# Score maxima read from two banks each by ScalarE and VectorE, and row tiles of 13 sequences turned by VectorE and DRAM

## The chip, the cores and the metric

The kernel runs on one core of a Trainium2 chip. The engines of a core are TensorE (PE), VectorE (DVE), ScalarE (ACT), GpSimd (POOL) and SyncE (SP, which here only issues DMAs); they run side by side and wait for each other by semaphores. The metric is the device time of one execution in microseconds (us), as the median of several runs; lower is better. Everything is computed in fp32.

## The reference

One post-norm decoder layer over 16 sequences of 512 tokens with 256 channels, and a context of 64 tokens with 128 channels for each sequence. `ln` is a layer norm without weights. Cut to what matters:

```python
def reference(x, ctx, ...):
    x = ln(x + hyena(x))            # gated long convolution, then an MLP of width 672
    x = ln(x + xattn(x, ctx))       # causal self-attention plus cross-attention, 16 heads of 16
    x = ln(x + ffn(x))              # 256 -> rank 64 -> 1024 -> rank 64 -> 256
    return x

def hyena(u):
    z = causal_conv3(rmsnorm(u) @ in_proj_w.T)
    x2, x1, v = split(z)
    y = (long_conv(x1 * v) + x1 * v * D_skip) * x2
    y = y @ out_proj_w.T + u
    zm = rmsnorm(y)
    return y + (gelu(zm @ l1_w.T) * (zm @ l2_w.T)) @ l3_w.T

def xattn(x, ctx):
    att  = where(causal, q @ k.T / 4, -inf)          # q, k, v from x, per head
    attc = qc @ kc.T / 4                              # qc from x, kc and vc from ctx
    return (softmax(att) @ v + softmax(attc) @ vc) @ Wp + bp

def ffn(x):
    return gelu((x @ U1) @ V1 + b1) @ U2 @ V2 + b2
```

Each softmax needs the maximum of its row of scores, over the allowed keys, before the exponentials are taken.

## The kernel before

**Two plans.** The kernel is written as a list of operations (`plan.op`), each with the engines that may run it, an assumed cost, an assumed latency of a DMA (`lat`), a priority, and the buffers that it reads and writes. `Plan.schedule` goes through an assumed time and gives each engine its order; a buffer is taken from its pool when its first operation starts. The table `RANKS` shifts priorities of single kinds of operations; `HOLD` and `STAY` weigh changes of the TensorE array's tiling. The result is a fixed order for each engine. On the chip every engine works through its own order, and a late operand holds up whatever comes behind it on that engine. A first plan (up to about 440 us) does the convolutions of all sequences; a second does everything else, sequence by sequence, overlapped.

**One sequence in the second plan.** `first_block` multiplies the convolution by its gate, projects it and makes the tile `y1`; the MLP follows, then a layer norm. `attention` makes keys, queries and values, the maxima, the sums, divides, projects and normalises. `ffn` is the last block. A tile of rows has tokens on its partitions, `[128, 4, 256]`; a matmul wants channels there. So each of the three blocks first turns its tile: `transposed` (L402) makes 8 PE transposes of 128x128 into two PSUM buffers of the pool `mm` (three in all), and ScalarE or VectorE copies each into the tile `xT` (three in all). Three turns a sequence: of `y1` (the trace names it y), of `x_` for attention and of `x_` for ffn (named xt, or early for every fourth or so).

**The tiling of the array.** PE runs either as 128*128 or cut into strips; a matmul of 128*32 uses a quarter of the columns, and four of them with different quarters run side by side. Score fills use 32*64 (eight side by side). Operations marked `flex` take the tiling that is on. Every fp32 matmul shows up in the trace as two. Transposes need 128*128.

**The scores.** There is one PSUM buffer `scores` of four banks, one for each head of a group; a sequence has four groups. For the maxima (`maxima`, L1472) a group makes three fills, (1, 0), (2 and the context of 3) and (3), by query block. For sequences 2 to 12 VectorE then adds the mask on the diagonal blocks in PSUM (L1548) and reduces all four banks there (L1580). For the five sequences of `COPIED` (0, 1, 13, 14, 15) ScalarE copies the whole fill to an SBUF tile `ex` (L1525), GpSimd masks it (L1532) and VectorE reduces it from there; in sequences 0, 1 and 15 the fill and the copy are made in halves (`HALVED_MAX`). The same buffer then holds the second computation of the scores, keys on the partitions, which ScalarE turns into exponentials (`sums`, L1611; context, L1688 on): five fills for a pair of groups and two for the context. The maxima of two groups are turned by PE (`max turn`, L1591) and added to the queries as an extra row (`shifted`, L1600).

**Other parts that the change touches.** The sums go to DRAM (`dn`), are divided by way of SP's queue and the SBUF tiles `nd` (three), and come back (L1765 on). `ffn` brings 256 channels to rank 64 (`rank`, L1852; both halves of the partitions get the same 64 ranks of all 512 tokens), then `hidden` (L1870) and GELU (L1876), 8 matmul groups of 64 rows. The context's values (`ctx v`, L1381) are made from a copy of the context side by side with itself (`twice`).

Of the kernel before, what the change touches and what calls it, by code (L numbers as in the profile page):

```python
# [27 lines left out]
    "context.sum ctx": -2000,  # L28
    "divided.num from": -400,
    "ffn.gelu": 4000,  # L30
    "ffn.hidden": -2000,
    "ffn.norm": 5000,
    "ffn.rank": -1000,
    "ffn.stats": 2000,
    "ffn.turn": -100,
    "ffn.wide": 4000,
    "first.load x": 2000,
    "first.out": -2000,
    "first.residual": -2000,
    "maxima0.max": -7000,  # L40
    "maxima1.copy": 1000,
    "maxima1.mask copy": -1000,
    "maxima1.max": -900,
    "mlp.down": 1000,
    "mlp.shift": -3000,
    "queries0.proj out": -320,
    "queries1.proj": 20,
    "queries1.proj out": -3000,
    "result.norm": 13000,
    "result.shift": 10000,  # L50
    "result.stats": 3000,
    "result.tokens": 14000,
    "shifted.max turn": 400,
    "shifted.shifted": 1000,
    "sums.exp": -1000,
    "sums.fill": -3000,
    "sums.sum": -2000,
    "sums.sum out": 2000,
    "values.ctx keys": 400,
    "values.ctx v out": 1000,  # L60
    "values.turn": -1000,
    "values.v": 100,
}
SLOT_OF = (1, 0, 2, 3)


class Buf:


    def __init__(self, cls):  # L70
        self.cls, self.seen, self.left, self.slot, self.t = cls, [], 0, None, None

# [27 lines left out]
class Plan:  # L100
# [55 lines left out]
    def matmul(self, out, weights, moving, **kw):  # L156

        rows, cols = self.now
        n = weights.shape[-1]
        for c in range(0, n, cols):  # L160
            cs = slice(c, min(c + cols, n))
            self.nc.tensor.matmul(out[cs], weights[:, cs], moving, **kw)  # L162
# [97 lines left out]
def decoder_layer(  # L260
# [60 lines left out]
    mask_qk = const.tile([P, P], F32, name="mask_qk")  # L321
    nc.gpsimd.memset(mask_qk, 0.0)
    nc.gpsimd.affine_select(
        out=mask_qk, in_=mask_qk, compare_op=ALU.is_ge, fill=NEG, base=0,
        pattern=[[-1, P]], channel_multiplier=1,
    )
# [100 lines left out]

    R8 = 8
# [5 lines left out]
    with ExitStack() as front:  # L434
# [40 lines left out]
        ramp_i = fp_.tile([P, P], I32, name="ramp_i")  # L475
        steps = fp_.tile([P, P], F32, name="steps")
        ramp = fp_.tile([P, P], F32, name="ramp")
        back = fp_.tile([P, 1], F32, name="back")
# [472 lines left out]
        u1_s = weights.tile([P, KD, 2, RANK], F32, name="u1_s")  # L951
        v1_s = weights.tile([P, NH // 2 * P], F32, name="v1_s")
        v2_s = weights.tile([P, D], F32, name="v2_s")
        v1_halves = v1.rearrange("r (p s n) -> s r p n", s=2, n=P)
        for n in range(2):
            half = bass.ts(n, RANK)
            fetch(u1_s[:, :, n, :], u1.rearrange("(k p) f -> p k f", p=P))
            fetch(v1_s[half, :].rearrange("r (p n) -> r p n", n=P), v1_halves[n])
            fetch(v2_s[half, :], v2)
        u1_s = u1_s.rearrange("p k s f -> p k (s f)")  # L960
# [110 lines left out]
        "row": tiles(kept, "row", 6, [P, T]),  # L1071
        "q": tiles(kept, "q", 11, [P, T]),
        "keys": tiles(kept, "keys", 5, [P, TC + T]),
        "kcs": tiles(kept, "kcs", 2, [P, 2, G, TC]),
        "ctx2": tiles(kept, "ctx2", 2, [CC, 2, TC]),
# [5 lines left out]
        "dk": dks,  # L1081
        "junk": tiles(kept, "junk", 1, [P, D]),
# [9 lines left out]
    for t in pool["maxes"]:  # L1092
        nc.gpsimd.memset(t, 0.0)

    plan = Plan(pool, 13890, 6870, nc, RANKS)
# [73 lines left out]
    def first_block(b, after):  # L1169
# [56 lines left out]
        if b:  # L1226
            scale_ops(y1, sq, p0, "ACT")
            zT = transposed(y1, lambda t: t, p0)
# [15 lines left out]
        for f in range(NF):  # L1244
            halves = []
            for w in (w_l1, w_l2):
                ps = Buf("mm")
                for k in range(KD):

                    def mm(e, f=f, w=w, k=k, ps=ps):  # L1250
                        plan.matmul(
                            ps.t, w[:, k, bass.ts(f, P)], zT.t[:, k, :], start=(k == 0), stop=(k == KD - 1)
# [24 lines left out]
        def mm_e(e, ps=ps):  # L1277
            for n, w in enumerate((w_l1, w_l2)):
                for k in range(KD):
                    for c in range(NT):  # L1280
                        plan.matmul(
                            ps.t[bass.ts(c, FE), bass.ts(n, P)], w[:, k, NF * P :], zT.t[:, k, bass.ts(c, P)],
# [32 lines left out]
    def attention(b, x_):  # L1315
# [3 lines left out]
        xT = transposed(x_, lambda t: t, p0)  # L1319
# [701 lines left out]
```

## Time and profile before

| | us |
|---|---|
| median of three runs (2019.52, 2025.77, 2025.89) | 2025.77 |
| the profiled execution, its own time | 2020.74 |
| its span, first to last instruction | 2018.6 |
| PE idle in 0 to 440 us (front plan) | 43.7 |
| PE idle in 500 to 1700 us | 4.3 |
| PE idle in 1700 to 1900 us | 5.2 |
| PE idle in 1900 to 2019 us | 17.7 |
| granted TensorE clock, mean | 0.992 |
| DMA: bytes moved, mean rate | 183.92 MB, 91 GB/s |

The idle times are a window's length less PE's busy time in it. The page gives the busy time of each engine, then 40 slices of the span, the DMA queues, the chain that ended last, and the costliest groups. In a group's line stand the source line, the engine, the operation, what is written and read, the count, the busy time in us, the mean of one in ns, and after the second bar the idle time before it. Nearly all matmuls have the line L162, a helper, so they are told apart by tile names. A "busy" PE holds overlapping and modelled ends; the start of one piece to the start of the next is the better measure of its cost. From 500 to 1700 us the kernel is in a steady state, in which a sequence takes 103.8 us.

### The profile page before, as it was taken

The page shows a single profiled execution, that of the slowest core. Times are in us where ns is not written, and L with a number is a line of the kernel's source. Part 1 is how long each engine was busy: PE and PEld are TensorE (multiplying, and loading weights), DVE is VectorE, ACT ScalarE, POOL GpSimd, SP SyncE. Part 2 cuts the span into 40 slices and gives each one's busy share as a digit, 9 for nine tenths or more (in the row PEclk, how much of TensorE's full clock was granted, in tenths as well). Part 3 has the DMA queues.
Part 4 walks back from the last instruction along what each step waited for, and adds up shares of the span by engine and source line. Part 5 has one row for each costly group of instructions (what it writes and reads, how often), then busy time and mean ns, then how long its engine had stood idle before and what let it go on. Part 6 is the DMA issues. An engine that isn't in the chain of part 4 may idle for free. (4 is left out here: it accounts for less than half of the span.)

```text
span 2018.6 us, 63455 instructions
## 1 busy us (share of the span) xinstructions
PE 1946.6 (96%) x28134; PEld 864.7 (43%) x28134; DVE 1320.4 (65%) x1907; ACT 1046.4 (52%) x1478; POOL 767.2 (38%) x1036
## 2 busy tenths in 40 slices
PE   7999978999999999999999999999999999999997
PEld 4445645444444443434343434343434343434442
DVE  7987542556576757676767667676767575656564
ACT  6863521566536362636363545444444546656774
POOL 7685622243423242414242423333332324424442
PEclk9999989999999999999999999999999999999999
DMA  5375871031304131313132222222231313131200
GB/s 191 123 212 172 274 256 48 13 104 38 116 21 133 29 121 41 113 50 112 51 102 60 94 69 81 82 74 89 61 102 52 106 38 108 28 103 39 83 23 32
DMA packets 115043, 183.92 MB, mean 91 GB/s; under 512 B 13393, under 2 KB 62034, under 8 KB 114642
## 3 DMA queue, kind: packets, MB, share of 16 engines
q1 hardware_dynamic: 113234, 177.26, 27.9%
q8 instruction: 220, 3.60, 0.7%
q10 hardware_dynamic: 1536, 2.62, 0.4%
q14 instruction: 53, 0.43, 0.1%
HBM read 111.09 MB, written 68.76 MB: 89 GB/s over the span
## 5 line engine op out<-in xcount | busy, mean ns | idle before, releaser
L1611 ACT ACTIVATE ex<-scores 128x2048 f32<-128x2048 f32 (+1 forms) x228 | 362.7, 1607 | 181.3 <-PE scores L162 177.7
L1659 POOL TENSOR_SCALAR_AFFINE_SELECT ex<-ex 128x512 f32<-128x512 f32 x256 | 158.6, 634 | 498.9 <-ACT ex L1611 498.8
L162 PE MATMUL mm<-xT,w_l 128*32 128x512 f32 (+2 forms) x2940 | 316.5, 540 | 0.0
L1580 DVE TENSOR_REDUCE maxes<-scores 128x8 f32<-128x512 f32 (+4 forms) x264 | 311.1, 1220 | 4.5
L162 PE MATMUL scores<-keys,q 32*64 32x192 f32 (+5 forms) x5696 | 218.1, 407 | 9.5 <-ACT ex L1525 5.0
L162 PE MATMUL scores<-q,keys 32*64 32x256 f32 (+3 forms) x4480 | 179.9, 420 | 6.2 <-ACT ex L1611 4.8
L1548 DVE TENSOR_TENSOR scores<-scores,mask_qk 128x1024 f32<-128x1024 f32 x132 | 115.6, 875 | 106.1 <-PE scores L162 105.3
L162 PEld LDWEIGHTS scores<-keys,q 32*64 32x64 f32 x5696 | 102.9, 131 | 172.2 <-DVE maxes L1580 52.9
L162 PEld LDWEIGHTS mm<-xT,w_l 128*32 128x32 f32 (+1 forms) x2940 | 92.7, 111 | 184.6 <-issue 175.0
L162 PE MATMUL av<-ex,va 128*32 128x512 f32 (+3 forms) x2048 | 169.0, 437 | 0.1
L162 PE MATMUL mm<-w_l,gT 128*32 128x256 f32 (+1 forms) x2032 | 159.7, 381 | 0.0
L562 DVE SCALAR_TENSOR_TENSOR frow<-fmm,cw,frow 128x511 f32<-128x511 f32 x192 | 140.5, 743 | 26.0 <-ACT frow L554 21.7
L1580 DVE TENSOR_REDUCE maxes<-ex 128x4 f32<-128x512 f32 (+3 forms) x120 | 140.6, 1211 | 17.9 <-POOL ex L1532 13.7
L1804 POOL TENSOR_TENSOR nd<-nd,nd 128x1024 f32<-128x1024 f32 x30 | 71.2, 2373 | 204.5 <-DMA nd<-di 204.5
L1525 ACT COPY ex<-scores 128x1024 f32<-128x1024 f32 (+1 forms) x96 | 114.3, 1228 | 66.7 <-PE scores L162 55.9
L547 PE MATMUL fmm<-fx,inw 128*128 128x512 f32 x312 | 142.2, 598 | 0.0
L361 DVE COPY row<-av 128x512 f32<-128x512 f32 x66 | 45.6, 690 | 138.8 <-PE av L162 137.7
L1876 ACT ACTIVATE row<-mm,b_s 128x512 f32<-128x512 f32 x124 | 78.9, 685 | 102.4 <-PE mm L162 99.5
L162 PE MATMUL mm<-xT,wqc_s 128*32 128x512 f32 (+1 forms) x796 | 125.4, 595 | 0.0
L162 PEld LDWEIGHTS scores<-q,keys 32*64 32x64 f32 x4480 | 79.5, 131 | 98.6 <-ACT ex L1611 45.0
L162 PEld LDWEIGHTS mm<-w_l,gT 128*32 128x32 f32 (+1 forms) x2032 | 89.3, 117 | 68.8 <-issue 34.5
L1263 ACT ACTIVATE row<-mm 128x512 f32<-128x512 f32 x80 | 47.9, 599 | 123.7 <-PE mm L162 112.0
(201 smaller groups left out, 2954.6 us busy)
## 6 DMA issues: line engine op xcount, KB each, us to landing
dn<-row SPq DMA_DIRECT2D x120, 256.0 KB
keys<-dk SPq DMA_DIRECT2D x64, 256.0 KB
nd<-dn SPq DMA_DIRECT2D x30, 512.0 KB
nd<-di SPq DMA_DIRECT2D x30, 512.0 KB
fx<-hpad SPq DMA_DIRECT2D x28, 512.0 KB
early<-gates SPq DMA_DIRECT2D x16, 512.0 KB
early<-yconv SPq DMA_DIRECT2D x32, 256.0 KB
dk<-row SPq DMA_DIRECT2D x32, 256.0 KB
```

The source lines that it names most:

```text
L162: self.nc.tensor.matmul(out[cs], weights[:, cs], moving, **kw)
L361: nc.vector.tensor_copy(dst, src)
L547: nc.tensor.matmul(ps.t, inw[:, k, bass.ts(m, P)], xT.t[:, k, :], start=(k == 0), stop=(k == KD - 1))
L562: lambda e, lag=lag: nc.vector.scalar_tensor_tensor(t.t[:, lag:], ps.t[:, 0 : T - lag], cw[:, m, 2 - lag : 3 - lag], t.t[:, lag:], ALU.mul ...
L1263: lambda e, pa=pa, ge=ge: nc.scalar.activation(ge.t, pa.t, AF.Gelu_apprx_tanh),
L1525: lambda e, sc=sc, both=both, cols=cols: nc.scalar.copy(both.t[:, :, cols], sc.t[:, :, cols]),
L1548: nc.vector.tensor_tensor(diag, diag, mask, ALU.add)
L1580: nc.vector.tensor_reduce(dst, src, AX.X, ALU.max, negate=True)
L1611: lambda e: nc.scalar.activation(ex.t.rearrange("p (r n) -> p r n", r=HPG)[:, :, cols], sc.t[:, :, cols], AF.Exp, scale=scale),
L1659: lambda e, ex=ex, at=at: nc.gpsimd.affine_select(out=ex.t.rearrange("p (r n) -> p r n", r=HPG)[:, :, at : at + P], in_=ex.t.rearrange("p ...
L1804: lambda e, nums=nums, inv=inv: nc.gpsimd.tensor_tensor(nums.t, nums.t, inv.t, ALU.mult),
L1876: lambda e, f=f, s=s, bank=bank, dst=hT[s]: nc.scalar.activation(dst.t, bank(s), AF.Gelu_apprx_tanh, bias=b1_s[:, f : f + 1]),
```

## The change

1. **Turns.** `turned` (new) replaces `transposed` for the three tiles of sequences 2 to 14: VectorE turns 32x32 blocks into an `xT` tile, one DMA writes it to DRAM (`turns`), and four DMAs read it back so that each 32-channel strip lies on its partitions. The tokens of such a tile lie in runs of 32; `tokens` and `columns` give the matmuls the access pattern. The maxima's own turn stays on PE, since the last entry of `TURNED` is empty.
2. **Maxima.** All 16 sequences take one form. Of the four banks of a fill, ScalarE copies two to an `nd` tile, GpSimd masks them and VectorE reduces them from there; VectorE reads the other two in PSUM: it adds the mask on the way into a small tile `part`, takes the maximum of what is off the diagonal, and then reduces `part`. `declare_no_dep` lets both engines read at once, since the banks differ. No fill is halved any more. The order of the first fill is (0, 1).
3. **ffn.** `rank` gives each half of the partitions its own half of the tokens (256 columns in place of 512); `hidden` and GELU then work in pieces of 256 columns.
4. **Context values.** Half as many columns, no copy `twice`.
5. **Plan.** New `RANKS`, `HOLD` 13570 and `STAY` 8710 (before 13890 and 6870), other assumed DMA latencies; pool `row` 5 (before 6), `q` 10 (before 11), `part` new, `ctx2` gone.

```diff
+    def turned(src, view, prio):
+        dst, via = Buf("xT"), Buf("turns")
+        dst.by_rows = True
+        def blocks(e):
+            nc.vector.transpose(
+                dst.t.rearrange("p k n -> p (k n)").rearrange("p (e k c i) -> p c k e i", e=NT, k=KD, c=NT),
+                view(src.t).rearrange("p c (k e j) -> p c k e j", k=KD, e=NT),
+            )
+        def there(e):
+            nc.sync.dma_start(out=via.t, in_=dst.t.rearrange("p k n -> p (k n)"))
+        def back(e):
+            rows = via.t.rearrange("(a j) (e n) -> e j a n", j=SLOT, e=NT)
+            for q in range(NT):
+                part = dst.t[bass.ts(q, SLOT)].rearrange("p k n -> p (k n)").rearrange("p (a n) -> p a n", a=NT)
+                nc.sync.dma_start(out=part, in_=rows[q])
+        plan.op("blocks", "DVE", dve(KD * T), blocks, prio, r=[src], w=[dst])
+        plan.op("blocks to", "SP", 0.6, there, prio, r=[dst], w=[via], lat=1.9)
+        plan.op("blocks from", "SP", 2.4, back, prio, r=[via], w=[dst], lat=3.5)
+        return dst
...
+    def tokens(xT, k, c=None):
+        if not xT.by_rows:
+            return xT.t[:, k, :] if c is None else xT.t[:, k, bass.ts(c, P)]
+        t = xT.t.rearrange("p k n -> p (k n)").rearrange("p (a k c i) -> p k c a i", a=NT, k=KD, c=NT)[:, k]
+        return t if c is None else t[:, c]
...
-        "row": tiles(kept, "row", 6, [P, T]),
-        "q": tiles(kept, "q", 11, [P, T]),
+        "row": tiles(kept, "row", 5, [P, T]),
+        "q": tiles(kept, "q", 10, [P, T]),
+        "part": tiles(kept, "part", PARTS, [P, HPG // 2, 2 * P]),
...
-            zT = transposed(y1, lambda t: t, p0)
+            zT = (turned if b in TURNED[0] else transposed)(y1, lambda t: t, p0)
...
-        xT = transposed(x_, lambda t: t, p0)
+        xT = (turned if b in TURNED[1] else transposed)(x_, lambda t: t, p0)
...
-            for use in (((1, TC), (0, TC)), ((2, TC), (3, None)), ((3, 0),)):
+            for use in (((0, TC), (1, TC)), ((2, TC), (3, None)), ((3, 0),)):
...
+                plan.op(
+                    "half", "ACT", act(two * T), lambda e, sc=sc, half=half: reading(sc, e, nc.scalar.copy(half.t, sc.t[:, two:])),
+                    prio - 6, r=[(sc, 1)], w=[half],
+                )
...
+                plan.op("half mask", "POOL", 0.4 * blocks, masked, prio - 6, w=[half])
...
+                    reading(sc, e, nc.vector.tensor_tensor(to, on_diagonal(sc.t[:, here]), m, ALU.add))
+                plan.op("mask", "DVE", dve(blocks * two * P), mask, prio - 5, r=[(sc, 0)], w=[part])
...
-                        nc.vector.tensor_tensor(diag, diag, mask, ALU.add)
-                    plan.op("mask", "DVE", dve((2 if use[0][0] == 1 else 1) * HPG * P), masked, ps_ - 5, w=[sc])
...
-                plan.matmul(ps.t, u1_s[:, k, :], x2T.t[:, k, :], start=(k == 0), stop=(k == KD - 1))
+                for n in range(P // SLOT):
+                    half, cols = n // 2, bass.ts(n % 2, SLOT)
+                    if x2T.by_rows:
+                        to = ps.t[bass.ts(n, SLOT), 0:D].rearrange("p (c a i) -> p c a i", c=2, a=NT)
+                        moving = tokens(x2T, k)[:, 2 * half : 2 * half + 2]
+                    else:
+                        to, moving = ps.t[bass.ts(n, SLOT), 0:D], tokens(x2T, k)[:, bass.ts(half, D)]
+                    nc.tensor.matmul(to, u1_s[:, k, cols], moving, start=(k == 0), stop=(k == KD - 1))
...
-    COPIED = (0, 1, B - 3, B - 2, B - 1)
-    HALVED, HALVED_MAX = (0, 1, B - 1), (0, 1, B - 1)
+    TURNED = *(range(2, B - 1) for n in range(3)), ()
+    HALVED = (0, 1, B - 1)
```

VectorE's instructions per group in the new form, with the elements per partition: first fill: mask 512, off-diagonal 256, context 256, own 512 (these read PSUM or `part`), then from `nd` context 256, own 256 and 512; second fill: 256, 512, 256, 256, then 256 and 768; third fill: 256, 768, 256, then 1024.

## The prediction

> **What bounds the kernel now.** I read the page's busy line first, then the windows by stage, then the same window for the tile `scores` alone, then PE's timeline, then the groups by shape.
>
> ```profile
> PE 1946.6 (96%) x28134; PEld 864.7 (43%) x28134; DVE 1320.4 (65%) x1907; ACT 1046.4 (52%) x1478; POOL 767.2 (38%) x1036
> ...
> 500.00:1700.00 1200.00, 1195.73 (x18172) 496.00 (x18165) 809.04 (x1145) 572.58 (x734) 393.35 (x529) 1.00 0.26 79
> ...
> 1900.00:2019.00 119.00, 101.28 (x1662) 42.00 (x1646) 71.91 (x143) 76.28 (x105) 41.54 (x70) 0.97 0.09 29
> ```
>
> In the windows the columns are length, then busy time of PE, PEld, DVE, ACT and POOL. TensorE is busy for all but 4 us of the 1200 us in the middle; VectorE has 391 us free there, ScalarE 627. The other view, same window, `scores` alone:
>
> ```profile
> 500.00:1700.00 1200.00, 307.71 (x7104) 124.32 (x7104) 426.62 (x396) 269.93 (x154) 1.00 0.26 79
> ```
>
> `scores` is one buffer, so its writers and readers take turns: 307.7 + 426.6 + 269.9 = 1004 us, 84% of the stretch. With a hand-over on each side of a fill, this turn-taking (I call it the ring) is nearly as full as PE. A shorter PE alone would soon meet it. PE's timeline shows what a piece of work costs from its start to the next start:
>
> ```profile
> 916.88 1.07 PE L162 MATMUL mm<-wp_s,xT 128*32 128x256 f32 x16
> 917.76 0.61 PE L162 MATMUL av<-ex,va 128*32 128x256 f32 x8
> ...
> 922.08 1.09 PE L410 MATMUL mm<-ident,xt 128*128 128x128 f32 x8
> 923.10 1.12 PE L162 MATMUL scores<-keys,q 32*64 32x320 f32 x32
> 924.15 1.07 PE L162 MATMUL mm<-xT,wk_s 128*32 128x512 f32 x8
> ...
> 942.67 0.64 PE L162 MATMUL mm<-wcv_s,ctx 128*32 128x256 f32 x8
> 943.24 0.66 PE L410 MATMUL mm<-ident,y 128*128 128x128 f32 x4
> 943.73 0.60 PE L162 MATMUL mm<-wp_s,xT 128*128 128x256 f32 x2
> 944.17 0.60 PE L410 MATMUL mm<-ident,y 128*128 128x128 f32 x4
> 944.61 0.60 PE L162 MATMUL mm<-wp_s,xT 128*128 128x256 f32 x2
> 945.13 1.12 PE L162 MATMUL scores<-q,keys 32*64 32x384 f32 x32
> ...
> 976.61 1.92 PE L162 MATMUL mm<-xT,u_s 128*32 128x512 f32 x16
> 978.35 1.90 PE L162 MATMUL mm<-xT,w_l 128*32 128x512 f32 x16
> ```
>
> **PE, removed.** (1) Turns. Sequences 2 to 14 lose their three tile turns: 39 tiles of eight transposes. Eight take 1.02 us (922.08 to 923.10), four take 0.49 and 0.44 (943.24, 944.17). 39 x 1.02 = 39.8 us. From below 39 x 0.88 = 34; from above by the busy unions of the three groups at L410 (28.0 + 18.4 + 10.6 us for 192 + 120 + 64, 0.152 each) 312 x 0.152 = 47. (2) Changes of the array's tiling. Two full-width pieces take 0.44 us before another full one, 0.52 before a 32*64 fill (944.61): 0.08 us for a change. A turned tile no longer pulls the array to 128*128: 39 x 0.1 = 4 us, between 0 and 8. (3) `rank`: 16 matmuls of 512 columns, 1.74 us (976.61 to 978.35), become 16 of 256, 0.88 us (916.88 to 917.76): 16 x 0.86 = 13.8 us; if the new form needs 1.05, 11. (4) `ctx v`: 0.57 us (942.67 to 943.24) for 8 of 256 columns becomes 8 of 128; 32 such take 0.90 us from 960.55, so 0.23 and a change: about 0.32. 16 x 0.25 = 4 us, between 0 and 5.
>
> **PE, added.** (5) `hidden` (16 x 512 in 1.02 us, 981.23 to 982.25) streams the same columns in twice as many matmuls. Fills of 16 x 512 (900.31 to 901.35) and 32 x 256 (912.05 to 913.10) take 1.04 and 1.05 us: I take 0; by the longest fill in the chain's list (1.20 us against 1.13) 64 x 0.1 = 6 us. (6) A by-rows tile is streamed in runs of 32 elements, which no row shows. Nearest: L664 streams 32 columns in runs of 8 in 199 to 201 ns, L756 48 contiguous ones in 207; at 0.85 ns a column (512 in about 0.435 us) 32 should take 193. 7 ns on 4 runs is 1.75 ns a run; 416 operations (20 of the MLP and 12 projections in 13 sequences) of two passes and 16 runs each would pay 23 us. I take 0, since such short matmuls show mostly their fixed part.
>
> Sum: 39.8 + 4 + 13.8 + 4 = 61.6 us. The last window has 18 us of idle PE, so the two turns and three ranks that fall there (4.6 us) give nothing: 57.
>
> **The maxima.** They use no PE, but they free the ring. Durations from the groups by shape: VectorE 0.41 us for 256 elements (the statistics at L1108), 0.69 for 512, 1.215 for 1024, so 0.155 fixed.
>
> ```profile
> L1548 DVE TENSOR_TENSOR scores<-scores,mask_qk 128x512 f32<-128x512 f32 x88 | 61.4, 698 | 65.8 <-PE scores L162 65.8
> ...
> L1580 DVE TENSOR_REDUCE maxes<-scores 128x4 f32<-128x1024 f32 x44 | 53.5, 1215 | 0.0
> ...
> L1525 ACT COPY ex<-scores 128x1024 f32<-128x1024 f32 x72 | 69.5, 1015 | 39.0 <-PE scores L162 28.2 <-issue 10.5 <-ACT row L363 0.3
> ```
>
> Before, VectorE held the buffer per group for 1.23 + 2 x 0.70 of masks and 2.29 + 1.75 + 2 x 0.69 + 1.215 + 0.68 of maxima: 9.95 us over three fills. Now it reads two banks: 0.70 + 0.41 + 0.41, 0.41 + 0.69 + 0.41, 0.41 + 0.95: 4.4 us, beside ScalarE's 1.02 a fill. That is 5.5 us a group, 22 us a sequence, off the ring. A sequence takes 103.8 us (the fill `scores<-q,kcs` starts at 834.03 and 937.84), PE wants about 99 after the change, the ring about 68. The later half on SBUF brings VectorE's total back to 10.0 us a group. The five sequences that were copied whole paid 7.27 (145.3 us over 20 groups): 20 x 2.7 = 55 us more. With 39 block turns (1.2 us by the 1024 row; a 32x32 turn has no row, I allow 0.7, the 512 row, to 3) and some 55 of 78 copies at 0.69 gone, VectorE ends near 1385 of 1965 us. ScalarE: 192 x 1.02 for 114 us of old copies, and 128 more GELU starts at about 0.3: +110 us, to 1155. GpSimd: 256 masks of 0.35 for 80 of 0.63: +40. I cost these at nothing, because PE's work covers them: in the steady stretch VectorE has 33 us in 100 free, ScalarE 52. Without cover the 55 us of the five sequences would show.
>
> The rows themselves first: a group's VectorE instructions go from 9 to 17, at 0.155 us fixed eight more are 1.2 us, 79 us in 64 groups, all inside the 10.0 above. [...]
>
> **What moves.** A turned tile now goes by VectorE, one write and four reads on SP's queue.
>
> ```profile
> 936.98 0.61 SPq L1453 DMA_DIRECT2D dk<-row  x1
> 941.28 0.32 SPq L1459 DMA_DIRECT2D keys<-dk  x1
> ...
> 963.66 0.61 SPq L1796 DMA_DIRECT2D nd<-di  x1
> ...
> 970.25 2.37 POOL L1804 TENSOR_TENSOR nd<-nd,nd 128x1024 f32<-128x1024 f32 x1 [4.07 <-DMA nd<-di]
> ```
>
> A 256 KB store lets the dependent read go 4.3 us later; a 512 KB read is used 6.6 us after its issue. So 1.2 + 4.3 + 1.3 (four issues at 0.32) + 4.3 to 6.6: 11 to 13 us from normed rows to turned tile, against 2.1 now (922.08 to 924.15). The issues (39 x 5 at 0.32 to 0.62, 62 to 121 us) go to SP, which mostly waits; but `blocks from` waits there for its store, with the key reads, the sums' stores and the divisions' reads behind it. A key read pushed late delays a maxima fill, a sums' store keeps a `row` buffer, of which one fewer is left. The plan books 2.5 and 5.9 us and can lay other PE work under it. I allow 2 us more PE waiting in all.
>
> 57 - 2 = 55 us. The profiled execution took 2020.74 us around a span of 2018.6; less 55 is 1965.7. The three runs shown were 2019.52 to 2025.89, median 2025.77, 5 us above it. I say 1966.
>
> **Rivals.** (A) The ring stays as full: ScalarE's copy queues behind other work, or lacks an `nd` buffer. For it: a division holds two of three `nd` from 950.84 to 973.98, 23 us twice a sequence, and half a fill needs 1.02 + 0.35 + 1.1 there before the next can be copied. If holds stay near 3.3 us a fill, the ring keeps its pace and PE idles where it was relieved: 2021, no change. Against: only half of the time, and the hold would be 2.5 us even then. 6%. (B) PE's costs of (5) and (6) are real, and the low ends of (1) to (4): 34 + 11 - 6 - 23 = 16, or half-way 30: 1991. Still faster. 10%. (C) Slower: the 9 to 11 us of added latency before the keys' projection is not covered. For it: the first use comes 0.1 us after the copies now, and keys, maxima and shifts follow. Price: 13 sequences by what is exposed; it decides from 57 / 13 = 4.4 us. With 6 us: 78 - 57 = 21 slower, 2042. Against: in the 17 us after 922.08 the list has projections, sums and `out` of another sequence, and the ring has gained 22 us a sequence. 14%.
>
> **Chances.** Main case 70%, A 6, B 10, C 14. About 0.3%, 6 us, can be told from no change here: faster 80%, same 6%, slower 14%. Range: upward 75 + 6 (PE's waits for L1525's copies) gives 1940; downward 16 gives 2005. I say 1938 to 2004.
>
> **What would show it.** No L410 turns between about 500 and 1800 us; PE still above 98% busy there; fills of `scores` in the maxima about 3 us apart when PE allows, not 4.6 to 5.5; the 512-column rows unchanged at 0.43 us a pass. Wrong: PE waits for `xT` from DMA, or `scores` fills waiting for ACT or `nd`; DVE above 90% in a window.

## The result and the profile after

The changed kernel takes **2114.57 us** (median of 4 runs, 2104.94 to 2117.21) against 2025.83 for the kernel before, run on the same chip: ratio 1.0429, 95% interval 1.0381 to 1.0477. It is 89 us slower. The forecast was 1966 us, with 80% on faster; both the sign and the range were wrong.

The page of the changed kernel, its busy time and three groups (busy us, mean ns of one | idle time before them and what ended it):

```profile
PE 1927.2 (91%) x28726; PEld 840.5 (40%) x28726; DVE 1359.1 (64%) x2493; ACT 1114.0 (53%) x1649; POOL 815.9 (39%) x1196
...
L158 PE MATMUL mm<-xT,w_l 128*32 128x512 f32 (+2 forms) x2874 | 322.4, 555 | 63.9 <-DMA xT<-turns 58.9
L1573 ACT COPY nd<-scores 128x1024 f32<-128x1024 f32 x192 | 194.6, 1014 | 347.1 <-PE scores L158 303.1
L1580 POOL TENSOR_SCALAR_AFFINE_SELECT nd<-nd 128x256 f32<-128x256 f32 x256 | 101.4, 408 | 591.9 <-ACT nd L1573 591.7
```

The window of 500 to 1700 us, all engines (length, then PE, PEld, DVE, ACT, POOL, the granted clock, DMA share and GB/s):

```profile
500.00:1700.00 1200.00, 1108.81 (x17927) 451.71 (x17908) 771.95 (x1443) 640.68 (x848) 436.11 (x652) 0.97 0.34 102
```

and the same window for the tile `scores` alone:

```profile
500.00:1700.00 1200.00, 296.90 (x6755) 118.35 (x6736) 176.63 (x346) 378.00 (x272) 0.97 0.34 102
```

Two things stand side by side. The ring did become emptier, as forecast: fill, VectorE and ScalarE hold the one buffer for 852 us of the stretch (296.9 + 176.6 + 378.0, and some of it overlaps now), before 1004 in turn. Yet PE, busy for all but 4 us of this stretch before, is idle for 91 us of it. Its waits, over the whole span (us in total, times, longest), and below them what the second one was before:

```profile
PE mm L158 <- DMA xT<-turns: 58.9, 9, 10.8
PE scores L158 <- ACT ex L1691: 31.4, 38, 2.1
PE av L158 <- POOL ex L1739: 16.7, 7, 4.2
...
PE scores L158 <- DMA keys<-dk: 6.2, 2, 5.7
```

```profile
PE scores L162 <- ACT ex L1611: 5.9, 7, 1.2
```

The nine waits on `xT<-turns` are `w_l`, the first matmul of the MLP: it is always the tile `y1`, one of three turned tiles in a sequence. In the steady part the last packet of the other two comes 7.2 to 9.6 us after the start of VectorE's block turn, about what the plan books; `y1`'s takes 15 to 21 us (11.9 in the first sequence of the stretch). One such case, on SP's timeline (start, us, queue, line, transfer), with an undisturbed tile at the end. VectorE's block turn (1.23 us) of the late tile began at 864.41, that of the other at 901.79:

```profile
858.99 0.60 SPq L1490 DMA_DIRECT2D dk<-row  x1
...
860.82 0.50 SPq L1862 DMA_DIRECT2D di<-sums  x1
866.68 0.34 SPq L1496 DMA_DIRECT2D keys<-dk  x1
...
871.34 0.38 SPq L430 DMA_DIRECT2D turns<-xT  x1
879.41 0.32 SPq L1496 DMA_DIRECT2D keys<-dk  x1
881.91 1.74 SPq L436 DMA_DIRECT2D xT<-turns  x4
...
903.05 0.32 SPq L430 DMA_DIRECT2D turns<-xT  x1
905.71 1.75 SPq L436 DMA_DIRECT2D xT<-turns  x4
```

The tile was ready to store at 865.64. SP stood at the next entry of its queue, `keys<-dk` (by the order of the queue, for the store of 858.99), then had five more issues ahead of the turn's own store, 5.70 us late. The reads went out 10.57 us after that store (2.66 for the undisturbed tile). Another `keys<-dk` stood in front of them, but what they waited for was their own store: its semaphore was complete at 881.89. The same holds for the `y1` tiles of all 13 sequences: the reads start 0.02 us after the store has landed. SP's wait there, over the whole span:

```profile
SPq L436 <- DMA turns<-xT: 117.8, 38, 9.2
```

So a late tile is late in two places. In the steady part its store is issued 2.1 to 5.7 us late (at once in the first sequence), and then lands 7.4 to 10.6 us after its issue (3.2 in the first sequence, 2.6 undisturbed). The second part is the larger. In this case SP issued six other transfers, 2 MB in all, between 866.68 and 870.70, just ahead of the store's 512 KB. The DMAs of 865 to 890 us moved 198 GB/s; at that rate 2.6 MB take 13 us (an estimate), which is nearly the 15 us from 866.68 to 881.89. The DMA row of the same stretch; a digit is the busy share of 0.625 us in tenths:

```profile
DMA  8562660437678976999755543910296999499600
```

And PE's side of it, first its timeline, then four windows around it (columns as above, granted clock third from the end):

```profile
886.36 1.93 PE L158 MATMUL mm<-xT,w_l 128*32 128x128 f32 x32 [10.79 <-DMA xT<-turns]
```

```profile
860.00:875.00 15.00, 15.00 (x248) 5.61 (x243) 7.35 (x11) 9.26 (x10) 5.95 (x9) 1.00 0.66 168
875.00:886.00 11.00, 0.57 (x8) 0.00 (x0) 2.22 (x5) 1.53 (x2) 4.33 (x4) 0.74 0.69 227
886.00:890.00 4.00, 3.64 (x64) 2.34 (x64) 0.29 (x1) 0.28 (x1) 0.00 (x0) 0.50 0.60 197
890.00:900.00 10.00, 10.00 (x152) 3.23 (x144) 8.60 (x17) 4.22 (x6) 1.18 (x3) 0.98 0.24 70
```

PE stands for 10.79 us, and when it starts again the granted clock is 0.50. The 32 matmuls of 886.36 take 1.86 us to the next start (0.87 at clock 1, the median of four such groups) and the 32 of the fill behind them 1.94 (1.05): about twice the time. By half of PE's 4.1 us of work in that low stretch (880.25 to 890.49), that adds 2.1 us to the 10.79, an estimate.

**Balance** from the two profiled executions. The span grew by 92.1 us (2018.6 to 2110.7). PE's idle time grew from 72.0 to 183.5 us: 111.5. The time that busy PE lost to the half clock (an estimate, half of its busy time in such stretches, by the two groups above) grew from 11.1 us in 6 stretches to 44.7 in 22: 33.6. So PE's work itself fell by 111.5 + 33.6 - 92.1 = **53 us**; the forecast had 61.6, of which it let 57 count. What was missed is 145 us of waiting and half clock.

### The profile page after: what moved, and what is told of

Read it like the earlier page. It is cut to its first block, busy times and chain, and to the rows that moved or that the text cites. A ratio compares the mean times of both kernels' runs of the same rounds, so it can differ in the third digit from the quotient of the medians.

```text
span 2110.7 us, 66232 instructions
## 1 busy us (share of the span) xinstructions
PE 1927.2 (91%) x28726; PEld 840.5 (40%) x28726; DVE 1359.1 (64%) x2493; ACT 1114.0 (53%) x1649; POOL 815.9 (39%) x1196
## 3 DMA queue, kind: packets, MB, share of 16 engines
q1 hardware_dynamic: 140658, 218.36, 33.6%
## 5 line engine op out<-in xcount | busy, mean ns | idle before, releaser
L158 PE MATMUL mm<-xT,w_l 128*32 128x512 f32 (+2 forms) x2874 | 322.4, 555 | 63.9 <-DMA xT<-turns 58.9
L1573 ACT COPY nd<-scores 128x1024 f32<-128x1024 f32 x192 | 194.6, 1014 | 347.1 <-PE scores L158 303.1
L1580 POOL TENSOR_SCALAR_AFFINE_SELECT nd<-nd 128x256 f32<-128x256 f32 x256 | 101.4, 408 | 591.9 <-ACT nd L1573 591.7
L1555 DVE TENSOR_REDUCE maxes<-nd 128x4 f32<-128x256 f32 (+4 forms) x384 | 246.1, 675 | 30.0 <-POOL nd L1580 29.9
L158 PE MATMUL scores<-keys,q 32*64 32x64 f32 (+4 forms) x5120 | 222.7, 447 | 8.2 <-DMA keys<-dk 6.2
L158 PEld LDWEIGHTS scores<-keys,q 32*64 32x64 f32 x5120 | 91.3, 135 | 169.8 <-issue 109.1
L1971 ACT ACTIVATE row<-mm,b_s 128x256 f32<-128x256 f32 x248 | 98.6, 478 | 97.2 <-PE mm L1959 88.7
L158 PE MATMUL mm<-xT,wqc_s 128*32 128x512 f32 (+1 forms) x1000 | 132.4, 622 | 5.5 <-DVE q L1448 5.5
L1594 DVE TENSOR_TENSOR part<-scores,mask_qk 128x256 f32<-128x256 f32 (+1 forms) x192 | 97.6, 508 | 51.9 <-PE scores L158 50.5
L583 ACT ACTIVATE frow<-fmm,cb,cw 128x512 f32<-128x512 f32 x96 | 74.2, 777 | 69.9 <-PE fmm L576 49.5
```

Source lines behind the costliest of these rows:

```text
L583: lambda e: nc.scalar.activation(t.t, ps.t, AF.Identity, bias=cb[:, m : m + 1], scale=cw[:, m, 2:3]),
L1555: inst = nc.vector.tensor_reduce(dst(), src(), AX.X, ALU.max, negate=negate)
L1573: "half", "ACT", act(two * T), lambda e, sc=sc, half=half: reading(sc, e, nc.scalar.copy(half.t, sc.t[:, two:])),
L1580: nc.gpsimd.affine_select(out=block, in_=block, compare_op=ALU.is_ge, fill=NEG, base=0, pattern=[[0, two], [-1, P]], channel_multiplier=1,)
L1594: reading(sc, e, nc.vector.tensor_tensor(to, on_diagonal(sc.t[:, here]), m, ALU.add))
L1971: lambda e, f=f, s=s, h=h, bank=bank, dst=hT[s]: nc.scalar.activation(dst.t[:, bass.ts(h, D)], bank(h)[:, bass.ts(s, D)], AF.Gelu_apprx_ta ...
```

## The experiments

For later: the kernel carries its own list planner, which gives each order an end on an assumed time axis. "Plan" below is the end of the second plan, read from each kernel's planner; the first plan's is 275.9 in all of them. Idle and clock loss are PE's, as in the balance.

| run | median us | ratio (95%) | plan | median - plan | idle | clock loss |
|---|---|---|---|---|---|---|
| before | 2024 to 2026 | 1 | 1743.5 | 282 | 72.0 | 11.1 |
| after | 2114.57 | 1.0429 (1.0381-1.0477) | 1716.3 | 398 | 183.5 | 44.7 |
| e1 all turns on PE | 2058.85 | 1.0169 (1.0142-1.0195) | 1769.4 | 289 | 111.9 | 17.7 |
| e2 `y1` on PE | 2098.91 | 1.0362 (1.0341-1.0383) | 1762.1 | 337 | 157.1 | 31.9 |
| e3 only `y1` by DRAM | 2368.76 | 1.1693 (1.1663-1.1723) | 2005.9 | 363 | 359.9 | 96.4 |
| e4 on ScalarE's queue | 2208.0 | 1.0907 (1.0890-1.0923) | 1834.4 | 374 | 240.1 | 74.3 |
| e5 no round trip | 2046.22 | 1.0105 (1.0089-1.0122) | 1716.3 | 330 | 130.5 | 27.7 |
| e6 round trip unwaited | 2087.92 | 1.0312 (1.0291-1.0333) | 1716.3 | 372 | 161.3 | 40.4 |
| e7 measured latencies | 2189.44 | 1.0807 (1.0779-1.0834) | 1858.2 | 331 | 223.1 | 62.6 |
| e8 matmul parts alone | 2050.49 | 1.0129 (1.0112-1.0146) | 1770.7 | 280 | 102.4 | 20.0 |
| e9 same, order kept | 2018.2 | 0.9974 (0.9964-0.9984) | 1743.5 | 275 | 78.0 | 14.7 |
| e10 before, no ranks | 2071.1 | 1.0237 (1.0217-1.0257) | 1803.1 | 268 | 100.4 | 21.8 |
| e11 before, after's ranks | 2140.85 | 1.0580 (1.0563-1.0598) | 1845.1 | 296 | 145.9 | 52.0 |
| e12 old latencies | 2099.94 | 1.0367 (1.0337-1.0397) | 1747.9 | 352 | 168.7 | 47.9 |
| e13 all turns, tuned | 2070.95 | 1.0236 (1.0212-1.0260) | 1691.0 | 380 | 149.9 | 36.1 |
| e14 no DRAM turns, tuned | 2012.75 | 0.9943 (0.9920-0.9965) | 1730.9 | 282 | 76.0 | 16.2 |
| e15 two turns, tuned | 2029.35 | 1.0017 (1.0003-1.0031) | 1703.5 | 326 | 110.4 | 25.6 |
| e16 before, tuned | 2015.8 | 0.9957 (0.9940-0.9974) | 1737.5 | 278 | 67.3 | 11.0 |
| e17 = e12, no round trip | 2028.49 | 1.0027 (1.0014-1.0039) | 1747.9 | 281 | 118.3 | 18.4 |
| e18 = e13, no round trip | 1975.67 | 0.9762 (0.9747-0.9776) | 1691.0 | 285 | 81.1 | 13.0 |

### Which turned tile, which queue (e1 to e4)

The first theory was that `y1`'s place in SP's queue is the whole loss. e1 turns nothing by DRAM, e2 all but `y1`, e3 only `y1`; e4 puts the turns on ScalarE's queue. e2, and e15 below, have six `row` buffers.

```diff
-    TURNED = *(range(2, B - 1) for n in range(3)), ()
+    TURNED = (), (), (), ()                                  # e1
+    TURNED = (), range(2, B - 1), range(2, B - 1), ()        # e2
+    TURNED = range(2, B - 1), (), (), ()                     # e3
...
-            nc.sync.dma_start(out=via.t, in_=dst.t.rearrange("p k n -> p (k n)"))      # e4, and the four reads
+            nc.scalar.dma_start(out=via.t, in_=dst.t.rearrange("p k n -> p (k n)"))
```

> The changed kernel with no tile turned by VectorE and DRAM (TURNED empty): all turns on PE again, everything else of the change kept. Theory Q (the turned tiles come late through SP's queue, and PE's fixed order waits for them): PE's waits for the turned tile (58.9 us in the page of after) and most of the idle time of 183.5 us go, about 42 us of turns come back: 2000 to 2030 us, near before. Rival M (the new maxima, with their copies and the shared nd buffers, are what is late; the waits for xT only show it): still 2080 us or more. Rival P (priorities and buffer counts chosen for another load): 2050 to 2100.

> The changed kernel with only the MLP's tile (y1) turned on PE, the tiles of attention and ffn still by VectorE and DRAM; row has 6 buffers in place of 5, since the plan finds no order with 5. Theory Q, in the form that it is the MLP's tile alone (its write and reads come in the thick of SP's queue, 15 to 20 us after the block turn, the two others after 7.3): the stalls before the MLP's first matmul go, 1980 to 2020 us. Rival Q2 (every turned tile costs, whichever it is): 2060 to 2090, two thirds of the loss kept. Rival M: 2090 or more.

> The changed kernel with only the MLP's tile (y1) turned by VectorE and DRAM, the tiles of attention and ffn on PE. Theory Q in the form of the MLP's tile: the loss stays, 2090 to 2140 us (a third of the saved turns, all of the stalls). Rival Q2: 2030 to 2060.

> The changed kernel with the five DMAs of each turned tile issued by ScalarE in place of SyncE, so that they wait in another queue than the sums, keys, gates and divisions; the plan books the same latencies. Theory Q (the place in SP's queue): a turned tile lands about 7 to 9 us after its block turn every time, 1980 to 2040 us, less what ScalarE loses by waiting for the store (39 x 2.3 us). Rival B (the DMA engines themselves are full in that stretch): landing still 15 us or more late, 2090 or more.

All four missed what the first theory said. e1 lies in rival P's range, e2 and e4 where M and B were placed, e3 in none. Without any DRAM turn the change still stands 34 us above the kernel before (e1); without `y1`'s it gains 16 us of 89 (e2); with `y1`'s alone it is the slowest of all (e3). No single tile explains that: in e3 PE waits 10 us for the turned tile and 220 us for the buffer `scores` (102.6 for exponentials, 63.3 for copies to `nd`, 54.2 for VectorE).

e4 does tell something of the late tile. On ScalarE's queue 9 of the 12 `y1` tiles after 500 us are stored within 0.11 us of the block turn's end and read as soon as the store has landed. Still their last packet comes 10.8 to 15.6 us after the turn's start in the steady part, not after 7.3. So the place in SP's queue is not all of the lateness; the traffic has a share, though mostly less than rival B's 15 us. Each of these edits alters costs that the planner sees, so each runs in **another order on every engine**. They compare orders as much as they compare turns, and the next experiments had to hold the order still.

### The same order, with and without the round trip (e5, e6)

An operation of the plan can keep its place and emit something else. In e5 `there` and `back` emit nothing; in e6 the reads land in a DRAM tile that nobody uses. The sequence of instructions on PE, DVE, ACT and POOL is that of the changed kernel.

```diff
         def there(e):
-            nc.sync.dma_start(out=via.t, in_=dst.t.rearrange("p k n -> p (k n)"))
+            pass                                             # e5
...
-                part = dst.t[bass.ts(q, SLOT)].rearrange("p k n -> p (k n)").rearrange("p (a n) -> p a n", a=NT)  # e6
+                part = spare.t[bass.ts(q, SLOT)].rearrange("p (a n) -> p a n", a=NT)
```

> The changed kernel, instruction for instruction in the same order on PE, DVE, ACT and POOL, with the turned tile's one store and four reads left out (195 DMA starts fewer on SP; the blocks stay where VectorE wrote them, so the values differ). Theory W (the 145 us of extra PE idle time and half clock hang on the turned tiles' way through DRAM, directly by 59 us of waits and the clock behind them, indirectly by what they push back in SP's queue): 1965 to 2020. Theory W' (only the 59 us named in the waits and their share of the clock, some 20 us, go): 2025 to 2050. Rival M (the new maxima and the order built around them cost the time): above 2070, with the waits of scores and av on ex unchanged near 48 us.

> The same order again; store and reads are all made on SP, but the reads land in a DRAM tile that nobody uses, so no one waits for them (values differ). It keeps the 195 starts, the waits in SP's queue for the store, and the traffic, and drops only the wait of the turned tile's readers. Wait alone: within 10 us of the kernel without the round trip. SP's queue as a block of its own: 20 to 60 us above it, with waits on keys and on ex (through late sums and divisions) as in the changed kernel.

The round trip costs 2114.6 - 2046.2 = **68 us** in this order. Only 27 of it is the wait of the turned tile's readers (2114.6 - 2087.9); the other 41 (2087.9 - 2046.2) stay when nobody waits, and come from 195 more starts in SP's queue, the waits there and the traffic, which were not separated (from 500 to 1700 us e6 moves 102 GB/s, as the changed kernel does). PE's waits in e6 show where those go:

```profile
PE scores L158 <- ACT ex L1692: 31.0, 38, 2.1
PE scores L158 <- DVE part L1601: 30.5, 9, 6.6
```

The 58.9 us of `xT<-turns` are gone and 30.5 us of another wait have come up in their place: the waits of a profile don't add up to what their removal is worth. SP's own waits in e6:

```profile
SPq L436 <- DMA turns<-xT: 140.4, 38, 8.4
...
SPq L1497 <- DMA dk<-row: 75.6, 18, 8.2
```

For 140 us SP stands at a read that waits for its own store, with everything behind it. The forecast for e6, 20 to 60 us above e5, holds. For e5 the range of W' (2025 to 2050) holds, but not its reason: it put the gain on the readers' wait, which is the smaller part. And 20 us above the kernel before, with 51 us less work for PE by the balance, e5 also says that the round trip is only part of the loss. PE's waits for the exponentials are there as in the changed kernel: 31.1 us of `scores` and 21.4 us of `av`, as rival M expected, though its time (above 2070) was wrong.

### Telling the planner the measured latency, and the matmul parts alone (e7, e8)

e7 changes `lat=1.9` to 5.9 and `lat=3.5` to 7.5 in `turned`. e8 is the kernel before with the new `rank`, `ctx v` and `hidden`, and its own maxima, ranks, pools and latencies.

> The planner is told 5.9 us for the store and 7.5 us for the reads instead of 1.9 and 3.5 (8 us more, what the late third tile measured); everything else as changed, the order is newly planned. If a too short booking is the cause: 1980 to 2040, xT<-turns under 20 us. If the latency costs wherever it is placed, or the order is fragile: 2090 or more.

> The kernel before with the change's TensorE parts alone: rank in strips (13.8 us forecast), ctx v in strips (4 us), hidden in halves with 128 more GELU starts (0), all turns by TensorE, the old maxima, the old ranks, offsets, pools and latencies. If PE's work is worth its time on this path: 2003 to 2012 (18 us less). If the ring of scores takes it back: 2018 to 2026. If every newly planned order is worse than one for which the ranks were chosen: above 2030.

Both were planned anew and both lost, each in its slowest range. In e7 the wait on `xT<-turns` is still 42.1 us (under 20 was expected if short booking was the cause). Its plan ends 142 us later and its time is 75 us longer, so that the gap between them falls from 398 to 331: the latency told as measured makes the plan truer and the kernel slower. e8 is the more telling: it takes 18 us of work from PE by the forecast (10 by the balance, in its own order), changes on the other engines only the split GELUs and the missing `twice`, and takes 24 us more. Its waits in the changed order:

```profile
PE scores L168 <- ACT ex L1686: 20.6, 23, 2.4
PE scores L168 <- ACT ex L1571: 17.4, 14, 2.2
```

### The order by itself (e9, e10, e11)

e10 and e11 have the operations of the kernel before in other orders (where the plan may choose an engine or a tiling, it chooses again); e9 does the opposite, new instructions in the old order (the planner is given the old costs, `twice` emits nothing; sequences 12 to 15 keep the old `rank`, because there the plan reuses a bank between two GELUs).

```diff
-    plan = Plan(pool, 13890, 6870, nc, RANKS)
+    plan = Plan(pool, 13890, 6870, nc, {})                   # e10
+    plan = Plan(pool, 13570, 8710, nc, RANKS)                # e11, with the changed kernel's RANKS
```

> The kernel before with its own planned order kept, and under it rank in strips and hidden in halves for the sequences 0 to 11 and ctx v in strips for all 16: the planner is given the old costs, so every piece of work stands where it stood, and only its instructions change. Work removed: 12 x 0.86 + 16 x 0.25 = 14.3 us (rank measured 0.90 us in the changed kernel, so 13.8). Theory R (PE's work is worth its time, and what costs is the newly planned order): 2009 to 2016. Rival S (the full ring of scores takes back what PE saves): 2021 to 2030. Rival C (the hidden halves and split GELUs cost more than they are shown to): above 2030.

> The kernel before with the table of ranks empty: the same work to the instruction, in another order. Theory R: 2045 to 2110, with PE's busy time within 10 us of before and the difference in idle time and half clock. If the order is of little weight: within 12 us of before.

> The kernel before, the same work again, planned with the changed kernel's ranks and its two offsets for a change of the tiling (13570 and 8710). Theory R: 2045 to 2130, since they were chosen for other work. If the order is of little weight: within 12 us of before.

With the same operations, the order alone is worth 47 us (e10) and 116 us (e11); the second is more than the whole change lost, and above theory R's range. Neither order was chosen for this work, so they show how far an order can go, not what the changed kernel's cost. In e11 the fills wait for VectorE to give back the ring:

```profile
PE scores L152 <- DVE maxes L1570: 49.8, 21, 3.8
PE scores L152 <- ACT ex L1601: 14.4, 22, 2.2
```

e10's PE is busy for 1974.0 us, 27 more than before and not "within 10"; 11 of these are the half clock, the rest was not taken apart. e9 is faster than before, by 3 to 7 us of the 14 removed; it falls between theory R (2009 to 2016) and rival S (2021 to 2030). In its trace PE's idle time is 6.0 us more and the half clock takes 3.6 more; of the ring only the waits of `scores` on `maxes` show it, 4.3 us for 2.0. With the order held, and the old maxima, PE's work was worth some two fifths of its time.

### Is the planner's end the measure? (e12 to e18)

In the table, the kernels without DRAM turns take 268 to 296 us more than their plan, whatever their order. That is close to the first plan's 275.9. The kernels with DRAM turns take 326 to 398 more. e12 gives the changed kernel the old latencies: 4.0 us for all five transfers of the sums and divisions, where the change had told the planner 1.7, 1.7 and 1.1 us for three of them and 5.7 for the other two, and 3.5 for the keys (3.4). For e13 to e16 I searched new ranks and offsets until the planner's end fell: e13 for the whole change, e14 without DRAM turns, e15 with the MLP's tile on PE, e16 for the kernel before. e17 and e18 are e12 and e13 with the round trip left out as in e5, the order on PE, DVE, ACT and POOL the same.

```diff
-                prio, r=[ysb], w=[(dn, (n, g % 2))], lat=1.7,        # e12; den, inverse, num likewise; keys 3.5
+                prio, r=[ysb], w=[(dn, (n, g % 2))], lat=4.0,
...
-    plan = Plan(pool, 13570, 8710, nc, RANKS)
+    plan = Plan(pool, 52347, 716, nc, RANKS)                 # e13, with its own RANKS
+    plan = Plan(pool, 37793, 61276, nc, RANKS)               # e14, TURNED empty
+    plan = Plan(pool, 112552, 410, nc, RANKS)                # e15, TURNED as e2
```

> The changed kernel with the latencies of before told to the planner for the sums, divisions and keys (4.0 and 3.5 us); ranks and all else as changed. The planner's end goes from 1716.3 to 1747.9, 32 us later. If the shortened latencies mislead it: at or below the changed kernel all the same, 2060 to 2110, so that time minus plan falls from 398 to 360 or less. If they don't matter and the planner's end does: 2130 to 2160.

> The whole change, the latencies of before, and ranks and offsets searched anew until the planner's end is 1691.0 (52 us below the kernel before, 25 below the changed one). If the order alone was wrong: 1691 + 283 = 1974, within 20. If what the plan doesn't see of the DRAM turns (a wait of 27, a queue of 41 us) stays: 2030 to 2060. If the planner's end says nothing: above 2080.

> The change without the DRAM turns (all turns by TensorE; new maxima, rank, ctx v and hidden as changed), the latencies of before, ranks and offsets searched anew until the planner's end is 1730.9, 13 us below the kernel before. If an order's worth is read from the planner's end plus some 283 us: 1999 to 2027, near 2014. If the new maxima cost time in any order: above 2040.

> The change with the MLP's tile of each sequence turned by TensorE and the other two through DRAM, six row buffers, the latencies of before, ranks and offsets searched anew: the planner's end is 1703.5. If only the third tile is late: 1703.5 + 283 = 1986, 1972 to 2000, with little waiting on xT<-turns. If any tile by DRAM brings what the plan doesn't see (350 us and more above the plan, as in five of six such kernels): 2040 to 2085.

> The kernel before, the same work, with ranks and offsets searched as for the tuned versions: the planner's end goes from 1743.5 to 1737.5. If the planner's end plus 283 us holds: 2008 to 2033, near 2020, 6 us less than before; then of the 12 us of the tuned version without DRAM turns at least half are the change's parts.

> The order of the changed kernel planned with the old latencies (planner's end 1747.9), with the turned tiles' store and reads left out as in e5 (values differ). If the shortened latencies are what is left in e5: 1747.9 + 268 to 296 = 2016 to 2044. If a plan with DRAM turns is late for another reason: 2065 or more, 318 us or more above the plan.

> The tuned order of the whole change (planner's end 1691.0, old latencies), store and reads left out (values differ). If with the round trip and the shortened latencies gone nothing is unseen by the plan: 1691 + 268 to 296 = 1959 to 1987, so that the round trip is worth 84 to 112 us in this order. If something else is late: 2009 or more.

e12 took 2099.9 us, in the range for latencies that mislead. Without DRAM turns the rule holds: e14 came in at 2012.75 where 2014 was expected, e16 at 2015.8 for 2020. e14 is **faster than both kernels**, by 0.6% against the one before, and so is e16 (0.4%), which changes no work at all. Their intervals overlap (0.9920 to 0.9965, 0.9940 to 0.9974), so that the change's maxima and matmul parts are worth anything beside a searched order is not shown.

With DRAM turns the plan misleads. e13 has the earliest end of all and takes 2071 us, between two of its ranges (2030 to 2060, above 2080); its first wait is the old one:

```profile
PE mm L247 <- DMA xT<-turns: 61.4, 12, 7.8
```

e15, with only the two tiles that land in time, is level with the kernel before (1.0017, above 1 by less than can be told here); both its ranges missed, one below and one above. Turned tiles no longer lead the waits, but the plan is still 326 us off, and the fills wait for GpSimd's part of the keys:

```profile
PE scores L244 <- POOL keys L1591: 25.4, 6, 5.8
PE scores L244 <- ACT ex L1777: 12.3, 16, 1.6
```

GpSimd copies the context's part of `keys` (0.23 us). It comes late because GpSimd's order has a division in front of it: before the wait of 5.79 us, GpSimd stands 10.70 us for the division's read `nd<-di`, divides from 753.23 on for 2.34 us and then makes the copies. So what is late is the divisions' traffic, which shares SP's queue with the turned tiles. How much of its delay is theirs was not measured.

e17 and e18 take the round trip and the changed latencies away, and both land where the kernels without DRAM turns do, 281 and 285 us above their plan. On the chip's own clock:

- **The round trip** costs 68 us in the changed order (e5), 71 in e12's (2099.9 - 2028.5) and 95 in the tuned one (2071.0 - 1975.7), whose plan ends earliest.
- **The order built on the changed latencies** costs 18 us against the one built on the old ones (e5 and e17, without the round trip) and 15 with it (the changed kernel and e12, whose intervals just overlap). The gap to the plan falls by more, 49 us (330 to 281), because the plan itself ends 32 us later. That the latencies by themselves make an order late is not shown: this is one pair of orders, and e1, with the changed latencies and no DRAM turns, is only 289 us above its plan.
- **Ranks and offsets** are worth 53 us between e17 and e18 (2028.5 - 1975.7), which do the same work with the same latencies.

These steps lead from e18 to the changed kernel: 1975.7 + 52.8 + 17.7 + 68.4 = 2114.6. From another order to start with, the shares would be others.

e18's waits have lost the line that led e13's:

```profile
PE scores L247 <- ACT ex L1777: 17.9, 22, 2.2
...
PE scores L247 <- DMA keys<-dk: 2.9, 2, 2.1
```

and PE is full again from 500 to 1700 us:

```profile
500.00:1700.00 1200.00, 1187.61 (x19834) 479.91 (x19830) 820.98 (x1536) 711.17 (x958) 472.51 (x709) 1.00 0.27 81
```

At 1976 us it shows what the change would be if a turned tile cost only VectorE's 1.24 us. It leaves out 195 transfers, so it is a bound and no version. Of those that compute the reference, e14 has the lowest median; one that keeps the DRAM turns and pays for them was not found. Not tried: a place in the plan for SP's entries that keeps a dependent read from standing before others, fewer transfers ahead of the turned tile's store, or the block turn's second half without DRAM.

## Why the prediction was wrong

**What held.** PE's terms: their sum was 61.6 us, the balance gives 53. `rank` takes 0.90 us (0.88 forecast, 1.74 before), `ctx v` 0.24 (0.32 forecast, 0.57 before), the halved `hidden` 1.02 (unchanged, as taken). The runs of 32 elements cost nothing that can be seen: from 500 to 1700 us 16 matmuls `mm<-xT,wqc_s` of 512 columns take 1.83 us from their start to the next in both kernels (median). VectorE ended at 1359 us (1385), ScalarE at 1114 (1155), GpSimd at 816 (807); none became the bound. The ring is relieved: from 500 to 1700 us the reads of a maxima fill end 1.5 us after it (median), where they took 3.2, and where PE allows the fills are 2.9 to 3.1 us apart (914.99, 918.06, 920.96), as forecast. VectorE's block turn takes 1.24 us (1.2). Of the signs that were named for being wrong, the first came: PE waits for `xT` from DMA.

**The step that failed** is "I allow 2 us more PE waiting in all", with its ground "the plan books 2.5 and 5.9 us and can lay other PE work under it". Measured: 111.5 us more idle time and 33.6 us more at half clock. Three things were wrong in it.

- *The queue and its traffic.* "`blocks from` waits there for its store, with the key reads, the sums' stores and the divisions' reads behind it" was written down and then priced at next to nothing. Starts, waits and traffic were 41 us (e6 against e5), more than the readers' own wait of 27. An undisturbed tile's last packet comes after 7.3 us, under the 11 to 13 forecast; the late one takes 15 to 21, because its store is issued up to 5.7 us late behind dependent reads and then needs 7.4 to 10.6 us to land among the transfers issued just before it.
- *The order.* The sum subtracted work from the old trace as if everything else would stay where it stood. It does not: planner, ranks, offsets and told latencies make a new order on every engine. With the round trip left out the changed order takes 2046 us (e5), 20 more than the kernel before, although PE has 51 us less to do; a searched order does the same work in 1976 (e18), where the forecast was 1966. So 71 us lie between the changed order and the best one found, 18 of them in the step from the old told latencies to the new, which the change lists and the sum never priced.
- *The clock.* The prediction has no term for it. In the trace of before, the stretches at half clock in which PE worked all lie in the first 415 us, and from 500 to 1700 us PE was idle for only 4.3 us. Waiting brought them into the middle: 33.6 us for 111.5 us more idle time.

**The rivals.** C ("the added latency is not covered", 14%) had the right side. It named the keys' projection; the exposed tile is `y1`'s, and its threshold of 4.4 us a sequence is just about what the waits show (58.9 / 13 = 4.5). Its 2042 us, from 6 us a sequence, left out the queue, the clock and the order. A did not occur as told: PE waited 0.2 us for copies to `nd`. But it did wait for the buffer `scores`, 31.4 us for the exponentials (5.9 before), which no rival named. B did not occur: PE's work fell by 53 us, where B had 16 to 30.

## What to carry to other kernels

In a kernel whose order is planned, a change of costs is also a change of order: hold the order and change the instructions, or hold the work and change the order, before saying what a part is worth; and an earlier end of the plan is no gain where the plan books a transfer shorter than it is. A round trip through DRAM on a queue that issues in order is priced by the transfers ahead of its store and by what stands behind the dependent read, as well as by its own latency: in this kernel 41 of its 68 us stayed when nobody waited for the tile (e6), and SP stood 117.8 us at the dependent reads. Where PE is full, price exposed waits at more than their length: in this kernel the half clock added 30% to the idle time.

## What the hardware showed

In both traces the granted clock of PE is either 1 or 0.5. In the changed kernel's it is low in 22 stretches: eight of 3.41 us, ten of 6.83, three of 10.24, and the last, which the end cuts. By the trace's clock records each starts a whole multiple of 3.413 us after the one before it (3 to 65 times it, within 1% of one). From 500 to 1700 us ten stalls of 2.9 to 10.8 us each brought a stretch of 3.4 to 10.2 us at half clock; by half of PE's busy time in them (2.95 to 6.19 us), each such stretch cost 1.5 to 3.1 us. A stall of 2.53 us (up to 990.00) brought none. In this kernel the half clock takes 33.6 us more than before, over a third of what the change lost.
